# Block 14's last down product: from ahead of the last block's projection to behind it

## The chip, the cores and the metric

The kernel runs on one core of one Trainium2 chip. A core has five engines with instruction queues of their own: TensorE (PE in the profile, its weight loads PEld), VectorE (DVE), ScalarE (ACT), GpSimd (POOL) and SyncE (SP), which here issues nearly all DMA transfers. Each engine takes its instructions in the order in which the program wrote them. The metric is the device time of one execution in microseconds (us).

## The reference

A transformer block with adaptive layer norm, on x of 8 sequences with 1024 tokens of 512 features, all in float32:

```
mod = silu(cond) @ Wada + bada        # six vectors of 512 for each sequence
xm  = layernorm(x, g1, be1) * (1 + sc_a) + sh_a
x   = x + gt_a * (causal attention, 16 heads of 32, of xm @ Wqkv) @ Wproj + bproj, gated
xm  = layernorm(x, g2, be2) * (1 + sc_m) + sh_m
h   = gelu(xm @ W1 + b1)              # 2048 features
out = x + gt_m * (h @ W2 + b2)
```

The change touches only the order of the last three lines for two neighbouring stretches of tokens: the second layer of the MLP (W2) of one, and the projection and second norm of the next.

## The kernel before

A block is one half of a sequence, 512 tokens; there are 16 blocks, 0 to 15, and block 15 is the last. In each block the kernel computes k, q and v, attention, the projection ("proj"), the modulated second norm ("mt"), four up steps ("u", one quarter of W1 each) and the down steps ("d", W2). Attention of block w and the linear layers of its neighbours run in one window w of a plan: lists of steps for each window, built in a loop (L245 to L287). Two strands share TensorE: attention, written by `attend`, and the linear steps, written as Python generators that stop wherever they would have to wait.

The big products use Strassen's scheme in Winograd's form: seven products of half size for eight. For W2 the pieces of the weight are A11, A12, A22 and the sums S1 to S4 of them, which are kept in DRAM; the pieces of the hidden layer are B11, B12, B21, B22, overwritten in place by their differences. One product of the down step reads four weight tiles (128 x 512) and is 16 calls of `matmul` (L212), each 8 matmul instructions in the profile; a product of an up step is four calls. `DOWN_ORDER` (L305) splits the seven down products into parts:

```
DOWN_ORDER = (("A11", "S1"), ("S4", "A12"), ("S2",), ("S3", "A22"))
```

Part 3, the last, first takes S3 with B11, adds the earlier partial sums (`u_d`, `p_d` in the profile), and stores token rows 256 to 511 of the block; then it takes A22 with B21, adds S3's result (`u3`, in the buffer `p1`) to it, gates it, adds it to the residual `xr` and stores rows 0 to 255 (L1399 to L1418).

The order of the work is written out ahead by a planner inside the program: it keeps a reckoned time for each engine (`now`), for when data is written (`written`) and when buffers are left (`left`). `work` (L1507) lets that strand write its next instruction whose reckoned wait is the shortest; side strands stand ahead of the main one in a tie, in the order in which they began. The main strand runs the plan's steps one after the other (`linear`); a step named "beside" is started as a side strand, and the main one goes on with the next step at once. When the last block's attention is done, `drain` writes all that is left.

Weights come through a ring of eight tiles (`RING`, `fetch`, L351): the order in which they are asked for is fixed by the plan (`order`, made of `pieces_of`), and tile i is asked for on SP's queue once tile i - 8 has been released. Linear products share three PSUM banks.

The last block's projection (`project_out`, L1131) runs over four row tiles of 128 tokens: four calls each, the one for the attention's last quarter being the last. Each tile is gated and added to the residual on DVE, and its norm follows at once (`normalize_tile`, L672: statistics on DVE, the root and the normalising on ACT, giving `hat_m`). "mt" (`modulated`, L725) then transposes the normalised tiles on TensorE (L771), scales and shifts them from PSUM (L775, L781) into `xm_m`, and makes the sums T1 to T4 for the up step (`t_m`). The first up step of block 15 doesn't begin before block 14's down steps are written ("down done").

The plan of the final window, with late the down parts 1 to 3 of block 14:

```
plan[NB] = late[:-1] + [("beside", late[-1]), ("proj", n), ("mt", n)] + mlp_steps(n)
```

Of the kernel before, what the change touches and what calls it, by code (L numbers as in the profile page):

```python
# [22 lines left out]
def kernel(  # L23
# [46 lines left out]
    NQ = HD // D  # L70
# [20 lines left out]
    NB = len(blocks)  # L91
# [149 lines left out]


    def mlp_steps(n):
        return [("u", n, i) for i in range(NQ)] + [("d", n, part) for part in range(4)]

    plan = {
        -1: [("mod", 0), ("mod", 1), ("sums", "k", 0), ("norm_columns_a",), ("at", 0)]
# [6 lines left out]
    for w in range(1, NB):  # L254
        n = w - 1
        m = mlp_steps(n)
        even = blocks[n][1] == 0
        rows_a = [("rows", blocks[n][0], "a")] if even else []
        rows_m = [("rows", blocks[n][0], "m")] if even else []
        own = m[:1] + ([("load_xa", w + 2)] if w + 2 < NB else []) + m[1:3]  # L260
        own += [("norm_a", w + 2)] if w + 2 < NB else []
        if w == NB - 1:
            steps = late[:2] + rows_a + [("proj", n), ("mt", n)] + late[2:]
            steps += rows_m + own + m[3:5] + [("load_xr", w)]
            late = m[5:]
        else:

            steps = late + [("v", w)] + rows_a + [("proj", n), ("mt", n), ("k", w + 1)]
            if w > 3 and blocks[w][1]:
                steps = late[:-1] + rows_a + [("proj", n), ("mt", n)] + late[-1:] + [("k", w + 1)]  # L270
            if w == 2:
                steps = late + [("v", w), ("k", w + 1)] + rows_a + [("proj", n), ("mt", n)]
            if w == 1:
                steps = rows_a + [("k", w + 1), ("proj", n), ("mt", n)]
            early_v = [("v", w + 1)] if w > 2 and not blocks[w][1] else []
            steps += early_v + [("q", w + 1)] + rows_m + own
            at = [("at", w + 2)] if w + 2 < NB else []
            if blocks[w][1] == 0:

                steps += m[3:5] + [("load_xr", w)]  # L280
                late = m[5:6] + at + m[6:]
            else:
                steps += m[3:5] + [("load_xr", w)] + m[5:6] + at
                late = m[6:]
        plan[w] = steps
    n = NB - 1
    plan[NB] = late[:-1] + [("beside", late[-1]), ("proj", n), ("mt", n)] + mlp_steps(n)  # L287

    kept_sums = {}
    column_source = {"k": (Wqkv, 1), "q": (Wqkv, 0), "v": (Wqkv, 2)}  # L290
# [11 lines left out]


    ORDER = ("A11", "A12", "S2", "S1", "S3", "S4", "A22")
    DOWN_ORDER = (("A11", "S1"), ("S4", "A12"), ("S2",), ("S3", "A22"))  # L305
    AT = {"A11": (0, 0), "A12": (1, 0), "A22": (1, 1)}
    FULL = {"A11": (0, 0), "A12": (1, 0), "A21": (0, 1), "A22": (1, 1)}
    RAW = ((0, 0), (1, 0), (0, 1), (1, 1))
# [5 lines left out]
    def pieces_of(step):  # L314

        kind = step[0]
        if kind == "mod":
            return [(Wada, step[1], kh, fh) for kh, fh in RAW]
        if kind == "gates":
            return [(Wada, GATES[step[1]][0], kh, fh) for kh, fh in RAW]  # L320
        if kind == "beside":
            return pieces_of(step[1])
        if kind == "proj" and not by_quarters(step[1]):
            return [(Wproj, 0, k) for k in range(NC)]
        if kind == "d":
            return [
                (W2, i, *AT[a]) if a in AT else (W2, i, a)
                for a in DOWN_ORDER[step[2]]
                for i in range(NQ)
            ]  # L330
        if kind == "sums":
            return [(*source_of(step[1:]), kh, fh) for kh, fh in RAW]
        if raw_step(step):
            return []
        if kind in ("k", "q", "v", "u", "proj"):
            w, i = source_of(step)
            return [(w, i, *AT[a]) if a in AT else (w, i, a) for a in ORDER]
        return []
# [942 lines left out]
    def down(n, part):  # L1281
# [85 lines left out]
        if part == 0:  # L1367
            yield [("g", n, 0), ("g", n, 1), "prepared", ("row", "gbm", n)], []
            for i in range(NTT):
                add_to(residual[n][:, i, :], gate_rows["gbm"], [("row", "gbm", n)], [("xr", n, i)])  # L1370
            written["rowgb free"] = due([("xr", n, i) for i in range(NTT)])
            combine(nc.vector, "B12", "B12", "B11")
            bank, ps = yield from product("B11")
            got["u1"] = stage("p1", "p1")
            copy_out(got["u1"], bank, ps, [key("u1")])
            bank, ps = yield from product("B12")
            got["u5"] = stage("p5", "u4")
            copy_out(got["u5"], bank, ps, [key("u5")])
        elif part == 1:
            bank, ps = yield from product("B22")  # L1380
            got["v3"] = stage("v3", "y", 2)
            y_key("v3", True)
            combine_out(got["v3"], bank, ps, got["u5"], [key("u5")], [key("v3")])
            combine(nc.vector, "B22", "B22", "B12")
            combine(nc.gpsimd, "B11", "B22", "B11")
            bank, ps = yield from product("B21")
            y = stage("y11", "y", 2)
            y_key("y11", True)
            combine_out(y, bank, ps, got["u1"], [key("u1")], [key("y11")])
            combine(nc.gpsimd, "B21", "B21", "B22")  # L1390
            settle(n, 0, 0, y, key("y11"))
        elif part == 2:
            bank, ps = yield from product("B22")
            u2 = got["u2"] = stage("u2", "u2")
            combine_out(u2, bank, ps, got["u1"], [key("u1")], [key("u2")])
            v3 = got["v3"]
            add_to(v3, u2, [key("u2")], [key("v3")])
            settle(n, 0, 1, v3, key("v3"))
        else:  # L1399
            u2, u5 = got["u2"], got["u5"]  # L1400
            bank, ps = yield from product("B11")
            u3 = stage("u3", "p1")
            combine_out(u3, bank, ps, u2, [key("u2")], [key("u3")])
            add_to(u5, u3, [key("u3")], [key("u5")])
            settle(n, 1, 1, u5, key("u5"))
            store(n, 1)
            if n == NB - 1:
                yield from last_product(u3, next_pieces=[next(at) for _ in range(NQ)])
                return
            bank, ps = yield from product("B21")  # L1410
            y = stage("y21", "y", 2)
            y_key("y21", True)
            combine_out(y, bank, ps, u3, [key("u3")], [key("y21")])
            settle(n, 1, 0, y, key("y21"))
            store(n, 0)
            for q in range(NQ):
                hTs.pop((n, q))
            written["down done", n] = 0.0  # L1418


    def perform(step):
        kind = step[0]
# [4 lines left out]
        elif kind == "gates":  # L1427
            yield from gates(step[1])
        elif kind == "columns_m":
            columns_of["m"] = norm_columns("m", 3, 4, O_G2, O_BE2)  # L1430
        elif kind == "load_xa":
            x_pre[step[1]] = load_x(step[1])
        elif kind == "load_xr":
            start(load_xr(step[1]))
        elif kind == "norm_a":
            key = f"a{step[1]}"
            normalize(x_pre.pop(step[1]), key, [("x", key)] * NTT)
        elif kind == "at":
            n = step[1]
            guards = [("m used", n - 3)] if n > 2 else [("v done", 0)] if n == 2 else []  # L1440
            start(modulated(f"a{n}", *columns_of["a"], blocks[n][0], guards))
        elif kind == "beside":
            start(perform(step[1]))
        elif kind == "sums":
            sum_weights(step[1:])
        elif kind == "mt":
            n = step[1]
            guards = [("v done", n + 1)]
            start(modulated(f"m{n}", *columns_of["m"], blocks[n][0], guards))
        elif kind == "k":  # L1450
            if step[1] != 3:
                yield [("free for k", step[1])], []
            yield from project_T(step, kTs, kvp, "kT", lambda: None)
        elif kind == "q":
            yield from project_T(step, qTs, act, "qT", lambda: projected.add(step[1]))
        elif kind == "v":
            yield from project_v(step)
        elif kind == "preps":
            prepared[0] = [preparation(), 0.0]
            written["prepared up"] = written["prepared"] = NEVER  # L1460
        elif kind == "rows":
            gate_broadcasts(*step[1:])
        elif kind == "proj":
            yield from project_out(step[1])
        elif kind == "u":
            yield from up(step)
        elif kind == "d":
            yield from down(*step[1:])
# [620 lines left out]
```

## Time and profile before

| | before |
|---|---|
| median of 3 runs | 3505.3 us (3503.61 to 3505.68) |
| the profiled execution | 3501.11 us |
| its span, first to last instruction | 3499.4 us |
| mean granted TensorE clock | 0.998 |
| TensorE busy | 3441.3 us, 98% |
| VectorE, GpSimd, ScalarE busy | 63%, 60%, 35% |

A row of the timeline has the start in us from the span's start, the length in us, the engine, the line of the program, the operation, out<-in by the program's names, the shape, how many instructions were merged, and in brackets how long the engine was idle before and what released it. SPq is the DMA queue of SP. The granted clock is the share of full speed that the throttle granted to TensorE. A time in the chain of waits is a stretch of the work that ended last. Matmuls overlap, so that the ends of rows are modelled, and differences between starts are the better measure.

### The profile page before, as it was taken

What the parts mean: (1) busy time and instruction counts of PE and PEld (TensorE: products, weight loads), DVE (VectorE), ACT (ScalarE), POOL (GpSimd) and SP (SyncE); (2) the same over time, 40 slices, a digit from 0 to 9 for tenths busy, and PEclk for the clock granted to TensorE, in tenths of its full rate; (3) what the DMA queues carried; (4) which work ended last, traced back from release to release, by engine and by line L of the source; (5) the groups of instructions that cost most, each with busy time, mean ns of one, the idle gap of its engine ahead of it and who ended that gap; (6) DMA issues with size and microseconds to landing.
All of it is one profiled execution on the core that took longest, in us unless ns stands there. A gap on an engine that the chain in (4) does not pass through costs nothing. (4 is left out here: it accounts for less than half of the span.)

```text
span 3499.4 us, 122173 instructions
## 1 busy us (share of the span) xinstructions
PE 3441.3 (98%) x55101; PEld 1750.9 (50%) x55101; DVE 2203.8 (63%) x2808; ACT 1212.8 (35%) x1272; POOL 2113.7 (60%) x2255
## 2 busy tenths in 40 slices
PE   8999999999999999999999999999999999999999
PEld 4444455445544555445554455544555445554555
DVE  5775675565666566565666656665666656656573
ACT  2335333342343513335232442333423333323521
POOL 3667847667366663767627676375762857628640
PEclk9999999999999999999999999999999999999999
DMA  6763444535535455363554535545455454543344
GB/s 213 237 188 104 137 125 139 147 104 171 147 118 158 119 162 149 103 182 116 152 152 127 159 116 152 153 137 146 130 154 143 130 144 132 154 126 98 104 134 140
DMA packets 335580, 498.84 MB, mean 143 GB/s; under 512 B 27724, under 2 KB 184460, under 8 KB 331476
## 3 DMA queue, kind: packets, MB, share of 16 engines
q1 hardware_dynamic: 334944, 490.99, 47.8%
q8 instruction: 434, 7.11, 0.8%
q14 instruction: 86, 0.70, 0.1%
q10 hardware_dynamic: 116, 0.03, 0.0%
HBM read 432.13 MB, written 56.69 MB: 140 GB/s over the span
## 5 line engine op out<-in xcount | busy, mean ns | idle before, releaser
L1911 POOL TENSOR_TENSOR pT<-pT,pT 128x256 f32<-128x256 f32 (+3 forms) x1254 | 1224.7, 1012 | 238.9 <-PE po L1810 123.9
L1782 ACT ACTIVATE pT<-st 128x2048 f32<-128x2048 f32 x288 | 541.1, 1879 | 1017.5 <-PE st L1770 886.3
L217 PE MATMUL bank<-w,hT 128*32 128x256 f32 x14336 | 822.1, 380 | 0.0
L1694 DVE TENSOR_REDUCE mx<-sc 128x4 f32<-128x2048 f32 (+3 forms) x383 | 663.3, 1753 | 200.5 <-PE sc L1679 194.7
L217 PEld LDWEIGHTS bank<-w,hT 128*32 128x32 f32 x14336 | 448.0, 110 | 389.8 <-issue 109.7
L217 PE MATMUL bank<-xm_m,w 128*32 128x256 f32 x8192 | 497.4, 381 | 2.3 <-ACT p_u L197 1.0
L217 PE MATMUL bank<-t_m,w 128*32 128x256 f32 x6144 | 384.0, 380 | 2.5 <-DVE qT L208 1.4
L217 PEld LDWEIGHTS bank<-xm_m,w 128*32 128x32 f32 x8192 | 255.5, 110 | 227.3 <-issue 56.6
L1787 POOL TENSOR_SCALAR_AFFINE_SELECT pT<-pT 128x512 f32<-128x512 f32 x256 | 177.3, 710 | 313.7 <-ACT pT L1782 313.3
L1679 PE MATMUL sc<-kT,qT 32*128 32x512 f32 (+3 forms) x3064 | 328.0, 520 | 3.1 <-DVE mx L1694 1.8
L1691 DVE TENSOR_TENSOR sc<-sc,mask 128x1024 f32<-128x1024 f32 (+1 forms) x160 | 162.8, 1017 | 255.2 <-PE sc L1679 210.8
L1810 PE MATMUL po<-pT,v 128*32 128x512 f32 (+3 forms) x3048 | 301.7, 490 | 2.5 <-POOL pT L1787 2.3
L1770 PE MATMUL st<-qT,kT 32*128 32x512 f32 (+3 forms) x3072 | 302.7, 487 | 0.0
L217 PEld LDWEIGHTS bank<-t_m,w 128*32 128x32 f32 x6144 | 188.9, 110 | 178.8 <-issue 49.8
L217 PE MATMUL bank<-xm_a,w 128*32 128x256 f32 x3968 | 241.6, 380 | 2.4 <-ACT p_k L197 1.1
L1679 PEld LDWEIGHTS sc<-kT,qT 32*128 32x128 f32 x3064 | 129.2, 183 | 182.4 <-issue 82.4
L208 DVE TENSOR_TENSOR hT<-bank,u_u 128x512 f32<-128x512 f32 x186 | 126.0, 686 | 127.2 <-PE bank L217 126.5
L217 PE MATMUL bank<-t_a,w 128*32 128x256 f32 x2944 | 182.3, 380 | 1.4 <-ACT qT L204 0.9
L1885 POOL TENSOR_TENSOR qT<-top,rec 128x512 f32<-128x512 f32 x61 | 79.8, 1309 | 170.7 <-DVE rec L1857 167.8
L217 PE MATMUL bank<-w,qT 128*32 128x512 f32 (+1 forms) x1824 | 175.4, 515 | 3.7 <-DMA w<-in_L_cond_Wproj_dram 3.7
L1199 ACT ACTIVATE hT<-hT,cols 128x512 f32<-128x512 f32 x256 | 164.7, 711 | 40.7 <-DVE hT L208 27.4
L217 PEld LDWEIGHTS bank<-xm_a,w 128*32 128x32 f32 x3968 | 123.9, 110 | 101.3 <-issue 16.9
(262 smaller groups left out, 3657.1 us busy)
## 6 DMA issues: line engine op xcount, KB each, us to landing
w<-in_L_cond_W_dram SPq DMA_DIRECT2D x384, 256.0 KB
w<-kept_up_S SPq DMA_DIRECT2D x256, 256.0 KB
w<-kept_down_S SPq DMA_DIRECT2D x256, 256.0 KB
w<-kept_qkv_S SPq DMA_DIRECT2D x180, 256.0 KB
w<-in_L_cond_Wqkv_dram SPq DMA_DIRECT2D x147, 256.0 KB
hat_a<-in_x_dram SPq DMA_DIRECT2D x64, 256.0 KB
xr<-in_x_dram SPq DMA_DIRECT2D x32, 512.0 KB
out_dram<-xr SPq DMA_DIRECT2D x31, 512.0 KB
```

What stands on the lines that cost most here:

```text
L208: nc.vector.tensor_tensor(out, src, other, op)
L217: nc.tensor.matmul(ps[r, :], columns, rhs, start=start, stop=stop, skip_group_check=True)
L1199: nc.scalar.activation(hT[:, i, :], hT[:, i, :], AF.Gelu, bias=cols[:, O_B1 + f : O_B1 + f + 1])
L1679: nc.tensor.matmul(sc[:, j, c0 : c0 + w], qTs[n][r, gg, ts(qt, P)], keys_of(n, kh)[r, gg, :w], start=True, stop=True, skip_group_check=True,)
L1691: nc.vector.tensor_tensor(place, place, shape_of.to_broadcast(place.shape), ALU.add)
L1694: nc.vector.tensor_reduce(maxima[n, gg][:, kh, qt, :], sc[:, :, c0 : c0 + w], axis=AX.X, op=ALU.max)
L1770: nc.tensor.matmul(st[:, j, c0 : c0 + w], kT[r, gg, ts(k % NTT, P)], qT[r, gg, TB - w :], start=False, stop=True, skip_group_check=True,)
L1782: nc.scalar.activation(pT[:, :, :used], st[:, :, :used], AF.Exp, scale=scale)
L1787: nc.gpsimd.affine_select(diagonal, diagonal, pattern=[[0, HPG], [1, P]], compare_op=ALU.is_ge, fill=0.0, base=0, channel_multiplier=-1,)
L1810: nc.tensor.matmul(po[r, TB - w :], v[:, k % NTT, g * P + j * hd : g * P + (j + 1) * hd], pT[:, j, c0 : c0 + w], start=(k == 0), stop=last ...
L1885: nc.gpsimd.tensor_tensor(qTs[n][:, g, :], top, rec, ALU.mult)
L1911: nc.gpsimd.tensor_tensor(into, into, pT[:, j, c0 : c0 + w], ALU.add)
```

## The change

The last part of the down step is cut in two: part 3 keeps S3 with B11, and a new part 4 has A22 with B21. For all blocks but 14 the two parts stand next to each other in the plan, as they did inside part 3; the lists in the plan that were cut before their last item are cut before their last two. In the final window part 3 of block 14 is started beside the projection of block 15, as before; part 4 is started as a side strand only when the projection has been written and "mt", the transposes behind the second norm, has been started. The order of the weight tiles follows: S3's four, Wproj's four, A22's four, then the up step's, where it was S3's, A22's, Wproj's, the up step's. `beside` takes a list of steps now, which `both` runs one after the other.

```
     def mlp_steps(n):
-        return [("u", n, i) for i in range(NQ)] + [("d", n, part) for part in range(4)]
+        return [("u", n, i) for i in range(NQ)] + [("d", n, part) for part in range(5)]
...
             if w > 3 and blocks[w][1]:
-                steps = late[:-1] + rows_a + [("proj", n), ("mt", n)] + late[-1:] + [("k", w + 1)]
+                steps = late[:-2] + rows_a + [("proj", n), ("mt", n)] + late[-2:] + [("k", w + 1)]
...
     n = NB - 1
-    plan[NB] = late[:-1] + [("beside", late[-1]), ("proj", n), ("mt", n)] + mlp_steps(n)
+    plan[NB] = late[:-2] + [("beside", late[-2:-1]), ("proj", n), ("mt", n), ("beside", late[-1:])] + mlp_steps(n)
...
-    DOWN_ORDER = (("A11", "S1"), ("S4", "A12"), ("S2",), ("S3", "A22"))
+    DOWN_ORDER = (("A11", "S1"), ("S4", "A12"), ("S2",), ("S3",), ("A22",))
...
         if kind == "beside":
-            return pieces_of(step[1])
+            return [at for of in step[1] for at in pieces_of(of)]
...
-        else:
+        elif part == 3:
             u2, u5 = got["u2"], got["u5"]
             bank, ps = yield from product("B11")
             u3 = stage("u3", "p1")
...
             store(n, 1)
+            got["u3"] = u3
+        else:
+            u3 = got["u3"]
             if n == NB - 1:
                 yield from last_product(u3, next_pieces=[next(at) for _ in range(NQ)])
                 return
...
+    def both(steps):
+        for step in steps:
+            yield from perform(step)
...
         elif kind == "beside":
-            start(perform(step[1]))
+            start(both(step[1]))
```

## The prediction

> **What bounds the kernel now.** I read the page first, then the chain of waits, then TensorE's timeline around the place that the change touches, then the same place on the other engines and the DMA queue.
>
> ```profile
> span 3499.4 us, 122173 instructions
> PE 3441.3 (98%) x55101; PEld 1750.9 (50%) x55101; DVE 2203.8 (63%) x2808; ACT 1212.8 (35%) x1272; POOL 2113.7 (60%) x2255
> ```
>
> TensorE is busy for all but 58.1 us of the span. An edit that only moves its work can gain no more than the idle time, and the slow time, of the places that it touches. Before the junction of blocks 14 and 15 the order of steps is the same in both kernels: every list in the plan that was cut before its last item is now cut before its last two, and flattens to the same order; the four-part cost of a block is the same sum. So I look at the junction alone. The chain of waits, in its columns start, length, what:
>
> ```profile
> 3350.57 40.52 PE bank L217 x624
> ...
> 3391.11 0.70 DVE y L208
> ...
> 3393.77 1.51 ACT hat_m L691 x2
> 3395.32 2.40 PE bank L771 x13
> 3397.73 97.74 PE bank L217 x1792
> ```
>
> The chain is on TensorE up to 3391.1, leaves it for the norm of the last row tile (DVE, then ACT) and comes back at 3395.3; then 97.74 us of matmuls without a gap lead to the end. Whatever is gained before 3397.7 moves all that follows by as much. TensorE's own timeline (start, length, what, idle before):
>
> ```profile
> 3350.20 27.12 PE L217 MATMUL bank<-w,hT 128*32 128x256 f32 x496
> 3376.97 14.09 PE L217 MATMUL bank<-w,qT 128*32 128x512 f32 x128
> 3390.99 0.33 PE L771 MATMUL bank<-ident,hat_m 128*128 128x128 f32 x1
> 3391.66 0.33 PE L771 MATMUL bank<-ident,hat_m 128*128 128x128 f32 x1 [0.33 <-ACT hat_m L691]
> 3394.62 0.33 PE L771 MATMUL bank<-ident,hat_m 128*128 128x128 f32 x1 [2.63 <-ACT hat_m L691]
> 3395.32 2.40 PE L771 MATMUL bank<-ident,hat_m 128*128 128x128 f32 x13 [0.38 <-ACT hat_m L691]
> 3397.66 2.79 PE L217 MATMUL bank<-xm_m,w 128*32 128x256 f32 x32
> 3400.27 1.90 PE L217 MATMUL bank<-t_m,w 128*32 128x256 f32 x32
> 3402.00 3.63 PE L217 MATMUL bank<-xm_m,w 128*32 128x256 f32 x64
> 3446.89 48.52 PE L217 MATMUL bank<-w,hT 128*32 128x256 f32 x896
> ```
>
> The first row is block 14's last four products with W2 (A12, S2, S3, A22), run through without a pause although the last two were started "beside" the projection; the second is the projection. Then TensorE waits three times for normalised tiles: 0.33 + 2.63 + 0.38 = 3.34 us. And it is slow afterwards. In the stretches below the columns are length, TensorE busy, granted clock, DMA share, GB/s:
>
> ```profile
> 3395.00:3396.00 1.00, 0.68 (x6) 1.00 0.01 2
> 3396.00:3397.00 1.00, 1.00 (x7) 0.51 0.00 0
> 3397.00:3398.00 1.00, 1.00 (x8) 0.50 0.00 0
> 3398.00:3399.00 1.00, 1.00 (x16) 0.50 0.00 0
> 3399.00:3400.00 1.00, 1.00 (x20) 0.78 0.00 0
> ```
>
> Time lost to the clock there: 0.49 + 0.50 + 0.50 + 0.22 = 1.71 us. Idle and slow time make 5.05 us, the most that filling this hole can bring.
>
> **The change, part by part.** *Splitting the last part of the second layer.* For blocks 0 to 13 and 15 nothing lies between the two halves, so their order is unchanged; I take zero, and the cover isn't work but identity of the two orders.
>
> *The second half (A22 with B21) leaves the stretch ahead of the projection.* The 896 matmuls of the last row are seven products of the same kind: 48.52 / 7 = 6.93 us; less the modelled tail of the row, 6.9 us, or 0.43 us for each of the product's 16 calls of eight matmuls. So the projection starts at 3376.97 - 6.9 = 3370.1 and ends at 3384.1 instead of 3391.0. That needs its data 6.9 us earlier:
>
> ```profile
> 3358.38 5.55 SPq L362 DMA_DIRECT2D w<-in_L_cond_W_dram  x4
> 3365.28 5.51 SPq L366 DMA_DIRECT2D w<-in_L_cond_Wproj_dram  x4
> 3372.19 2.11 SPq L362 DMA_DIRECT2D w<-in_L_cond_W_dram  x2
> 3377.80 2.20 SPq L1250 DMA_DIRECT2D out_dram<-xr  x2
> 3390.24 1.24 SPq L362 DMA_DIRECT2D w<-in_L_cond_W_dram  x2
> 3365.74 0.29 DVE L1866 TENSOR_TENSOR qT<-top,rec 128x128 f32<-128x128 f32 x1
> 3372.65 0.69 DVE L167 TENSOR_TENSOR xr<-xr,p_d 128x512 f32<-128x512 f32 x1
> ```
>
> The ring has eight slots, so a weight tile is requested when the tile eight places earlier is released. Today A22's four tiles are requested from 3358.4 to 3363.9 (behind S2's release) and Wproj's four from 3365.3 to 3370.8. The two groups change places in the order, so Wproj takes the first times. For the landing I take a bound: the last weight request before the hole ends by 3391.5, and the DMA share is 0.01 in 3395 to 3396, so a tile lands within some 4 us. Wproj is there by 3363.9 + 4 = 3367.9, 2.2 us ahead of need; the last quarter of the attention output is there at 3366.0, 4.1 us ahead; DVE has finished S3's additions at 3373.3, and the projection's first row tile comes out seven of sixteen calls after its start, near 3376.3. Nothing waits: zero, between the bounds 0 and 4 us. The weights of the following up layer lose: four of them are today requested behind A22's release (3372.2 onward) and now behind Wproj's, at the projection's last row tile, near 3381 to 3384. With 4 us they are there at 3388, and the first is needed after 3394. Zero.
>
> *The second half fills the hole.* The norm's chain depends on the projection alone, so it moves by 6.9 us with it:
>
> ```profile
> 3388.27 0.81 ACT L691 ACTIVATE hat_m<-xr,offset_m,rstd_m 128x512 f32<-128x512 f32 x1
> 3390.80 0.80 ACT L691 ACTIVATE hat_m<-xr,offset_m,rstd_m 128x512 f32<-128x512 f32 x1
> 3393.77 1.50 ACT L691 ACTIVATE hat_m<-xr,offset_m,rstd_m 128x512 f32<-128x512 f32 x2
> 3396.13 2.42 ACT L781 ACTIVATE xm_m<-bank,shiftm,gainm 128x512 f32<-128x512 f32 x3 [0.86 <-PE bank L771]
> 3399.30 0.69 DVE L167 TENSOR_TENSOR t_m<-t_m,xm_m 128x512 f32<-128x512 f32 x1
> ```
>
> The four normalised tiles come 1.9 us before the projection's end, and 0.6, 3.5 and 4.3 us behind it. The hole behind it is thus 4.3 us, and 6.9 us of A22 stand ready. In what order they are written is settled by the kernel's planner: it takes whichever thread waits least, the transposes' first in a tie. By its own reckoning of the norm the tiles come at -1.3, 1.6, 4.4 and 5.2 us of the projection's end, later than in the trace, so it writes one transpose, three calls of A22, a transpose, six calls, a transpose, one call, then transposes with two calls and four calls put where a PSUM bank is not yet free. The price of such mixing shows where block 14's transposes were mixed with W2 products:
>
> ```profile
> 3212.02 0.33 PE L771 MATMUL bank<-ident,hat_m 128*128 128x128 f32 x1
> 3212.28 0.64 PE L217 MATMUL bank<-w,hT 128*32 128x256 f32 x8
> 3212.85 0.33 PE L771 MATMUL bank<-ident,hat_m 128*128 128x128 f32 x1
> 3214.75 1.97 PE L771 MATMUL bank<-ident,hat_m 128*128 128x128 f32 x14
> ```
>
> 14 transposes take 1.97 us, 0.14 each. One transpose and one call take 3212.85 - 3212.02 = 0.83 us, 0.26 more than 0.14 + 0.43: each change of kind costs 0.13 us. From the projection's end to the first product with a sum (T2), the after kernel runs 16 transposes (2.25), 16 calls (6.9), the first up product (four calls, 1.73) and some ten changes of kind (1.3): 12.2 us. Today that stretch takes 3400.27 - 3390.99 = 9.3 us, with 6.9 us of A22 ahead of the projection: 16.2 us. **The gain is 16.2 - 12.2 = 4.0 us.** The same from the other side: 3.34 idle + 1.71 slow clock - 8 more changes of kind at 0.13 = 4.0. Bounds: 5.1 if there are no more changes than today; 3.0 if the transposes wait as much for free banks as today's thirteen (2.40 against 13 x 0.14 = 1.8, so 0.6) and the planner mixes three times more.
>
> *What the half's own outcome is queued with.* Its DVE work is three instructions (bank plus S3's result, times the gate, into the residual) of 0.69 us, 2.1 us in all. It stood in DVE's idle time ahead of the projection; now it stands behind the sums for the up layer (last today at 3399.30). The sums themselves stand ahead of it by the planner's times, so T2 isn't delayed: after hat 4.3 us behind the projection, four evictions and two sums end near 3394.5, and TensorE wants T2 at 3396.3. Up's first partial product reuses the buffer of S3's result, so its copy out waits for the first of the three, near 3396; the bank it frees is wanted two products later. Zero, at most 1 us. The store of rows 0 and 1 of block 14 now stands on the DMA queue behind four more weight requests and ahead of the next layer's; with eight tiles (eight products, 13.8 us) in hand nobody waits for it.
>
> **The rivals.** *The clock stays low (3503.0).* If the slow 3.4 us isn't due to this hole, only the idle time less the changes of kind comes back: 3.34 - 1.04 = 2.3. For it: no single pause is longer than 2.63 us, and TensorE worked for 1 us in between. Against it: the fall follows the pauses at once, within 0.7 us. The Trainium skill, "TensorE: Matmul & The Clock Gate", section "What's actually happening", says that the clock halves after an idle window of about 3.4 us and recovers after about 3.4 us of sustained work; the trace agrees with half and with the 3.4 us of recovery, but taken literally, a pause of 2.63 us should not have cost anything, and the loss would have another source.
>
> *It doesn't do what it says (3505.3).* If all transposes are written ahead of A22, TensorE's queue keeps its order: it waits 3.34 us as now and A22 follows behind, 6.9 us later. The stretch is 16.2 us in both. It would take a planner that sees no wait at the second and third tile; it reckons 1.6 us and 4.4 us, so I hold it unlikely.
>
> *Slower (3511).* The Wproj requests get behind the store of block 14's rows 2 and 3 on the DMA queue. That store waits for the addition at 3372.65 + 0.69, takes 1.1 us to issue (2.20 for two), and Wproj's first tile lands at 3374.4 + 4 = 3378.4, against 3370.1: 8.3 us of waiting, another fall of the clock (1.7) and 4.0 gained elsewhere make +6.0. It decides once the projection starts later than 3374.1. Against it: the requests are written as S2 is released, before the store's addition exists.
>
> **How the numbers follow.** The profiled execution took 3501.11 us (span 3499.4 and 1.7 around it); less 4.0 it is 3497.1. The median of the three runs is 3505.3, 4.2 us above the profiled one, so I forecast 3501.3. Chances: 0.72 for this, 0.08 for the clock that stays low, 0.09 for no effect, 0.05 for the late weights, 0.06 for a larger gain from something that the trace of before doesn't show. 0.2% is 7.0 us, about what a measurement of this kernel can tell from no change, and more than the 5.05 us that the hole holds: faster 0.06, same 0.89, slower 0.05. The likeliest case alone gives 3500.2 to 3502.3 and, with the 1 us by which the runs differ, 3499.2 to 3503.3. The range takes in no effect and a run 0.7 above it: 3499.0 to 3506.0.
>
> **What would show it.** Right: the profile shows the projection starting near 3370 straight behind S3; matmuls of bank<-w,hT between the transposes; TensorE's idle time in the junction under 0.5 us; a granted clock of 1.0 to the end; the T2 product near 3396.3. Wrong: an idle stretch ahead of the projection (weights or attention late), a new pause between the transposes and the up layer (DVE's queue), or a different order in an earlier block, which would show as a different instruction count or a shift before 3350.

## The result

| | before | after |
|---|---|---|
| median of 21 runs each | 3505.3 us (3499.37 to 3514.14) | 3500.46 us (3491.1 to 3504.99) |
| ratio | | 0.9983, 95% interval 0.9976 to 0.9989 |
| the profiled execution | 3501.11 us | 3492.33 us |
| its span | 3499.4 us | 3490.6 us |

The kernel became 0.17% faster by the ratio, which is 6.0 us, with an interval of 3.9 to 8.4 us; the medians lie 4.8 us apart. The forecast was a gain of 4.0 us and a time of 3501.3. On the page of the changed kernel the span is 8.8 us shorter and TensorE is busy for 3.3 us less:

```profile
span 3490.6 us, 122172 instructions
PE 3438.0 (98%) x55101; PEld 1752.9 (50%) x55101; DVE 2204.5 (63%) x2809; ACT 1211.8 (35%) x1271; POOL 2112.5 (61%) x2255
```

DVE has one instruction more and ACT one less, since one of the last transposed tiles (`xm_m`) is now scaled on DVE. That is at the junction: up to the place where A22's product stood, TensorE, DVE, ACT and GpSimd run the same instructions in the same order in both traces.

The chain of waits no longer leaves TensorE at the junction (start, length, what):

```profile
3346.26 33.59 PE bank L217 x496
3379.84 0.26 PE bank L771
3380.10 1.43 PE bank L217 x24
...
3388.07 98.60 PE bank L217 x1824
```

TensorE's timeline of the changed kernel shows what stands where DVE and ACT stood in the chain before:

```profile
3345.03 1.22 PE L1838 MATMUL bank<-pT,ones 128*32 128x512 f32 x8
3345.89 20.22 PE L217 MATMUL bank<-w,hT 128*32 128x256 f32 x368
3365.75 14.10 PE L217 MATMUL bank<-w,qT 128*32 128x512 f32 x128
3379.78 0.33 PE L771 MATMUL bank<-ident,hat_m 128*128 128x128 f32 x1
3380.03 1.50 PE L217 MATMUL bank<-w,hT 128*32 128x256 f32 x24
3381.47 0.33 PE L771 MATMUL bank<-ident,hat_m 128*128 128x128 f32 x1
3381.72 2.80 PE L217 MATMUL bank<-w,hT 128*32 128x256 f32 x48
...
3385.28 0.77 PE L771 MATMUL bank<-ident,hat_m 128*128 128x128 f32 x5
3385.98 1.07 PE L217 MATMUL bank<-w,hT 128*32 128x256 f32 x16
3386.98 1.09 PE L771 MATMUL bank<-ident,hat_m 128*128 128x128 f32 x8
3388.00 1.93 PE L217 MATMUL bank<-w,hT 128*32 128x256 f32 x32
...
3391.48 1.91 PE L217 MATMUL bank<-t_m,w 128*32 128x256 f32 x32
```

No row has an idle time in brackets, and the clock is full throughout (length, TensorE busy, granted clock, DMA share, GB/s):

```profile
3379.78:3391.48 11.70, 11.70 (x178) 1.00 0.51 161
```

To compare kernels I measure the **junction**: from the start of the last product with ones to the start of the first product with t_m. In the kernel before, the first mark is this row of TensorE's timeline:

```profile
3349.35 1.22 PE L1831 MATMUL bank<-pT,ones 128*32 128x512 f32 x8
```

Before: 3400.27 - 3349.35 = 50.92 us. After: 3391.48 - 3345.03 = 46.45 us. The junction gives 4.47 us. The two profiled spans differ by 8.8 us, and the other 4.3 us stood at the first mark already. They are no effect of the change, since up to there the instructions and their order are the same. The lead of the changed execution comes and goes on the way: 1.3 us at 146 us, 4.6 at 156, 1.4 at 2630 (the same matmul starts at 2629.99 and at 2628.65), 4.3 at the first mark. Its largest step shows how. The kernel before, first the stretch's granted clock (third figure), then its timeline:

```profile
146.50:149.90 3.40, 3.33 (x14) 0.51 1.07 245
```

```profile
146.57 1.21 PE L1649 MATMUL bank<-kT,qT 32*128 32x512 f32 x1 [2.19 <-DVE mx L1666]
156.00 0.40 PE L1758 MATMUL st<-mrow,minus_ones 32*128 32x384 bf16 x8
```

The changed kernel, the same stretch and the same instructions:

```profile
146.50:149.90 3.40, 3.40 (x22) 1.00 1.09 286
```

```profile
145.25 0.69 PE L1656 MATMUL bank<-kT,qT 32*128 32x512 f32 x1 [2.39 <-DVE mx L1673]
151.37 0.40 PE L1765 MATMUL st<-mrow,minus_ones 32*128 32x384 bf16 x8
```

One execution fell to half clock behind a pause of 2.2 us, the other didn't behind 2.4 us (the last section says why). Ahead of it they are 1.32 us apart at the same instruction, behind it 4.63. Single executions of one kernel differ by such events, so below single times are not compared, only junctions within a trace, and the medians of null_split, one_piece and late_turns, which were run ten or eleven times.

### The profile page after: what moved, and what is told of

It reads as the page before. It is cut to its first block, busy times and chain, and to the rows that moved or that the text cites. A ratio compares the mean times of both kernels' runs of the same rounds, so it can differ in the third digit from the quotient of the medians.

```text
span 3490.6 us, 122172 instructions
## 1 busy us (share of the span) xinstructions
PE 3438.0 (98%) x55101; PEld 1752.9 (50%) x55101; DVE 2204.5 (63%) x2809; ACT 1211.8 (35%) x1271; POOL 2112.5 (61%) x2255
```

## The experiments

| kernel | first mark | T2 product | junction, us | longest pause in it, us | half clock behind it |
|---|---|---|---|---|---|
| before | 3349.35 | 3400.27 | 50.92 | 2.63 | yes |
| null_split | 3348.72 | 3399.39 | 50.67 | 2.64 | yes |
| both_ahead | 3347.74 | 3399.51 | 51.77 | 2.63 | yes |
| behind_turns | 3344.40 | 3396.02 | 51.62 | 2.56 | yes |
| fill_3, two executions | 3352.70, 3355.88 | 3402.38, 3405.55 | 49.68, 49.67 | 1.61, 1.60 | no |
| fill_7 | 3356.32 | 3406.00 | 49.68 | 0.19 | no |
| old_loads | 3352.94 | 3400.89 | 47.95 | 1.30 | no |
| after | 3345.03 | 3391.48 | 46.45 | none | no |
| both_behind | 3351.05 | 3397.49 | 46.44 | none | no |
| one_piece | 3348.98 | 3394.89 | 45.91 | none | no |
| late_turns | 3357.79 | 3403.37 | 45.58 | none | no |

**The cut without the move.** In null_split only the plan's line differs from the changed kernel:

```
-    plan[NB] = late[:-2] + [("beside", late[-2:-1]), ("proj", n), ("mt", n), ("beside", late[-1:])] + mlp_steps(n)
+    plan[NB] = late[:-2] + [("beside", late[-2:]), ("proj", n), ("mt", n)] + mlp_steps(n)
```

> The part is cut in two as in the changed kernel, but both halves run ahead of the projection, as before: every engine gets the instructions of the kernel before in the same order. I measure the junction from the start of the last product with ones (bank<-pT,ones) to the start of the first product with t_m: 50.92 us before, 46.45 after. My theory (all of the gain is the filled hole) expects 50.9, with the half clock behind the hole again, and no difference in the median. Rival 1 (the half clock falls there by chance, wherever a free-running window happens to lie): 50.9 or 49.2. Rival 2 (the cut itself or the code's place brings something): a median some 4 us below the kernel before.

The expectation overlooked one thing: the second half now takes its tiles from the ring only after the projection has, so the last projection multiplies by A22's tiles and A22's product by Wproj's, and the output is not the block's. The instructions of the engines and their order are those of before, and only the times are used here. Junction 50.67 us, ratio 1.0007 (0.9998 to 1.0016). The cut itself brings nothing; rival 2 falls.

In both_ahead part 3 takes all eight tiles, which puts both the tiles and their requests where they were before:

```
-    DOWN_ORDER = (("A11", "S1"), ("S4", "A12"), ("S2",), ("S3",), ("A22",))
+    DOWN_ORDER = (("A11", "S1"), ("S4", "A12"), ("S2",), ("S3", "A22"), ())
...
-            got["u3"] = u3
+            got["u3"], got["at"] = u3, at
...
-            u3 = got["u3"]
+            u3, at = got["u3"], got["at"]
```

and the plan's line is that of null_split.

> Cut in two as in the changed kernel, but both halves ahead of the projection and the weight tiles asked for in the old order: the instructions of the kernel before, in its order, on every engine. Theory: the hole and the half clock behind it are there again, junction (from the start of the last product with ones to the first product with t_m) 50.9 us against 46.45 of the changed kernel. Rival (the half clock behind the hole is chance): 49.2 us.

Its timeline, and behind it the stretches with the granted clock as the third figure:

```profile
3393.01 0.47 PE L771 MATMUL bank<-ident,hat_m 128*128 128x128 f32 x1 [2.63 <-ACT hat_m L691]
```

```profile
3395.00:3397.00 2.00, 2.00 (x13) 0.50 0.00 0
3397.00:3399.00 2.00, 2.00 (x24) 0.53 0.00 0
```

The hole and the half clock are there again. Here the half clock lasted twice as long, 6.8 us in place of 3.4, and began during the pause; the junction is 51.77, so what the hole costs varies by about 1 us (50.67 to 51.77 in the three kernels with the old order). That the half clock comes by chance at this place, the first rival, isn't borne out: four kernels of four with this pause show it.

**The hole filled, nothing moved.** fill_7 is the kernel before with a strand of useless calls:

```
+    def filler(calls):
+        yield [], [BANK]
+        bank = lin_bank()
+        for i in range(calls):
+            if i:
+                yield [], []
+            matmul(
+                banks[bank][:, :HB], qTs[NB - 1][:, 0, :P], gate_rows["gm"][:, :HB],
+                i == 0, i == calls - 1, [], bank,
+            )
+        live[bank] = False
+        left["l", bank] = now["PE"]
...
+        elif kind == "fill":
+            start(filler(step[1]))
...
-    plan[NB] = late[:-1] + [("beside", late[-1]), ("proj", n), ("mt", n)] + mlp_steps(n)
+    plan[NB] = late[:-1] + [("beside", late[-1]), ("proj", n), ("mt", n), ("fill", 7)] + mlp_steps(n)
```

> The kernel before, with seven useless calls (56 matmuls on data that is there, into a free bank, read by nobody) written as a side strand beside the transposes: they fill the wait for the norm and move nothing. If the half clock is the price of the hole, the clock stays at 1.0 and the stretch from the projection's end to the first product with t_m falls from 9.28 to about 8.2 us although TensorE has 3.0 us more to do; junction 49.8. If the low clock has another source, it stays, and the stretch grows to 9.9 us; junction 51.5.

From fill_7's timeline, and its granted clock from the projection's end to T2:

```profile
3399.92 1.93 PE L217 MATMUL bank<-row_gm,qT 128*32 128x256 f32 x32
3402.30 1.89 PE L771 MATMUL bank<-ident,hat_m 128*128 128x128 f32 x13 [0.19 <-ACT hat_m L691]
```

```profile
3397.97:3406.00 8.03, 7.81 (x107) 1.00 0.42 127
```

8.03 us for that stretch against 9.28 before, though TensorE has 3.0 us more to do. The norm comes no sooner: the last 13 transposes start 18.36 us behind the projection's start (3402.30 - 3383.94), and 18.35 us in the kernel before (3395.32 - 3376.97). From there T2 follows in 3.70 us, against 4.95 before. What went is the half clock, and it was worth 1.25 us. fill_3, the same with three calls, asks how long a pause it takes:

> The kernel before with three useless calls in place of seven: the first 1.3 us of the wait are filled, some 1.5 us ahead of the third transpose and 0.4 us ahead of the fourth stay idle. What it tells apart: whether a pause of 1.5 us is enough to bring the half clock (so far the junction showed it in four looks of four with a pause of 2.6 us, and in none of five without a pause above 0.2 us). With the half clock the junction is about 50.9 us, without it 49.2. I expect 49.2: no half clock.

> The same kernel once more, since a free-running window may lie differently: 49.2 us without the half clock, 50.9 or more with it. If one look has it and the other not, the pause of 1.5 us is near the bound and chance decides.

The first execution's timeline, and its stretch from the projection's end to T2:

```profile
3397.98 0.33 PE L771 MATMUL bank<-ident,hat_m 128*128 128x128 f32 x1 [1.61 <-ACT hat_m L691]
```

```profile
3394.35:3402.38 8.03, 6.01 (x74) 1.00 0.37 120
```

Both executions have a pause of 1.6 us and full clock, and the same 8.03 us: with 2.0 us still idle the junction is that of fill_7, since the norm's chain sets when the last 13 transposes can start, 18.35 us behind the projection's start here too. The expected 49.2 took all of the 1.71 us of slow time for lost; 1.25 us were. At full clock TensorE waits for a part of that time anyway: in fill_3 the first up product starts 1.87 us ahead of T2, not 1.73, and a gap of 0.2 us lies between two of the 13 transposes.

**Behind the projection, but not in the hole.** In behind_turns part 4 of block 14 waits for a mark that is set when the transposes are written:

```
+            if n == NB - 2:
+                yield ["transposed"], []
...
+        if key == f"m{NB - 1}":
+            written["transposed"] = 0.0
...
+    written["transposed"] = NEVER
```

> The changed kernel, but A22's product may only be written once all transposes are: it is behind the projection and doesn't fill the hole. My theory: TensorE waits 3.3 us for the norm as before, nothing is gained, junction 49.2 to 50.9 us (without and with the half clock). Rival (the gain comes from the projection's earlier start, or from its weights' earlier requests): 46.5.

Its timeline, and a stretch of its granted clock:

```profile
3382.77 0.47 PE L771 MATMUL bank<-ident,hat_m 128*128 128x128 f32 x1 [2.56 <-ACT hat_m L691]
3383.47 3.04 PE L771 MATMUL bank<-ident,hat_m 128*128 128x128 f32 x13 [0.23 <-ACT hat_m L691]
3386.44 8.02 PE L217 MATMUL bank<-w,hT 128*32 128x256 f32 x128
```

```profile
3386.00:3388.00 2.00, 2.00 (x19) 0.50 0.00 0
```

The projection starts as early as in the changed kernel, and the pause is 2.56 us as before; 13 transposes take 3.04 us and A22 7.85 by the starts (3394.29 - 3386.44) instead of 6.9, both in part at half clock. The junction is 51.62, 0.7 above the expected range, with a half clock that lasted 6.8 us as well. An earlier projection, with its weights asked for earlier, is worth nothing alone: the gain is the filling.

**More behind the projection.** both_behind moves S3's product too:

```
+    plan[NB] = late[:-2] + [("proj", n), ("mt", n), ("beside", late[-2:])] + mlp_steps(n)
```

> S3's product goes behind the projection too: 13.8 us of work stand ready for a hole of 4.3 us behind the projection. Theory: only the hole can be filled, so the second 6.9 us bring nothing, junction 46.0 to 47.0 us. Rival 1 (each product moved behind gains as much again): 43 or less. Rival 2 (the projection now comes before its attention rows and weights, which were 4.1 and 2.2 us ahead of need in the prediction's sum): 48 or more, with an idle stretch ahead of the projection.

The row of its timeline behind the last transpose:

```profile
3387.11 8.84 PE L217 MATMUL bank<-w,hT 128*32 128x256 f32 x160
```

46.44 us, the changed kernel's 46.45. Twelve calls of S3 fill the hole, as twelve of A22 did in the changed kernel; the other four and all of A22 run behind the transposes. Both rivals fall; the projection doesn't wait either, although it starts 6.9 us earlier still.

**The old order of requests.** old_loads has the changed kernel's plan with both_ahead's `DOWN_ORDER` and taking of tiles.

> The changed kernel's order of matmuls with the old order of weight requests: S3's four tiles, A22's four, Wproj's four, so that Wproj's come 6.9 us later and A22's eight slots are held until behind the projection. Theory: Wproj's requests leave some 5 us ahead of use at first and arrive just in time or up to 1 us late: junction 46.4 to 47.5. Rival (the exchange of the requests is needed, the prediction's slower case): the projection waits 2 us or more, junction above 48.4, half clock behind it possible.

From its timeline, and from its chain of waits:

```profile
3377.03 12.22 PE L217 MATMUL bank<-w,qT 128*32 128x512 f32 x112 [1.30 <-DMA w<-in_L_cond_Wproj_dram]
```

```profile
3372.32 4.66 DMA w<-in_L_cond_Wproj_dram
```

The projection's first two calls run at 3373.65, 0.88 us each, and the third waits until 3377.03, 1.6 us late by the starts; the junction is 47.95, between the two expectations. So the exchanged order of requests is part of the change's gain, 1.5 of the 4.47 us, but its lack doesn't turn the sign.

**Better mixtures.** one_piece starts A22's strand ahead of the transposes':

```
+    plan[NB] = late[:-2] + [("beside", late[-2:-1]), ("proj", n), ("beside", late[-1:]), ("mt", n)] + mlp_steps(n)
```

> A22's product is started ahead of the transposes, so that it runs in one piece and the 16 transposes follow. If each change of kind costs 0.13 us, eight changes fewer save 1.0 us, and waits for banks and for the last eviction give some back: 45.9 to 46.7 us for the junction against 46.45. Rival (the mixing is what hides the evictions): transposes, evictions and sums stand in a row behind the product, and the junction is 47.5 or more.

late_turns leaves the plan and lets the first transpose wait for all four tiles:

```
-            yield [("hat", key, 0), *guards], [BANK]
+            whole = range(NTT) if key == f"m{NB - 1}" else range(1)
+            yield [*(("hat", key, t) for t in whole), *guards], [BANK]
```

> The changed kernel, but the first transpose waits for the fourth normalised tile, so that TensorE changes between A22's calls and transposes six times, not ten, and two groups of calls still cover the evictions. By 0.13 us for a change: 0.5 us less than the changed kernel, junction 45.9 us; in the median no difference from it that can be told, about 0.998 of the kernel before. Rival (a change of kind costs nothing when both kinds stand ready): 46.4.

From the timeline of late_turns:

```profile
3392.24 5.54 PE L217 MATMUL bank<-w,hT 128*32 128x256 f32 x96
3397.71 1.09 PE L772 MATMUL bank<-ident,hat_m 128*128 128x128 f32 x8
3398.73 1.07 PE L217 MATMUL bank<-w,hT 128*32 128x256 f32 x16
3403.37 1.91 PE L217 MATMUL bank<-t_m,w 128*32 128x256 f32 x32
```

one_piece has 45.91 and 0.9984 (0.9975 to 0.9993), late_turns 45.58 and 0.9978 (0.9968 to 0.9987). Fewer changes of kind are cheaper: late_turns was written with four of them, not the six of the expectation, so six less than the changed kernel, and saved 0.87 us, 0.15 for each. In one_piece eight changes fewer saved only 0.54 us: the up layer's first product starts 2.07 us ahead of T2 and not 1.73, which the expected waits for the evictions would do; no run takes that apart. By one trace each both beat the changed kernel; by the medians neither can be told from it.

## Why the prediction was right

*The start of the projection* came 6.9 us earlier as summed: from the first mark to its start 27.62 us before (3376.97 - 3349.35), 20.72 after (3365.75 - 3345.03).

*The written order* is the predicted one call for call: a transpose, three calls, a transpose, six, a transpose, one, five transposes, two calls, eight transposes, four calls.

*The stretch from the projection's end to T2* was put at 12.2 us and took 11.70. The mis-sized term is the transposes, 0.14 us each or 2.25 in all: eight of them with one change of kind take 1.02 us and five with one change 0.70, which makes 0.11 each, 1.8 in all. The row from which the 0.14 came (14 in 1.97 us) holds a change of kind too, and a wait for the eviction of a bank, which the kernel before shows on the weight loads of its last four transposes:

```profile
3216.06 0.42 PEld L771 LDWEIGHTS bank<-ident,hat_m 128*128 128x128 f32 x4 [0.23 <-ACT xm_m L781]
```

With 11.70 the working gives 16.2 - 11.7 = 4.5 us, the junction's 4.47.

*The two losses*, idle time and half clock, are told apart by fill_7 and fill_3: with the pause cut to 1.6 us or less, the clock stays full and the stretch is 1.25 us shorter although changes of kind were added. So the sum from the other side, 3.34 + 1.71 - 1.04 = 4.0, came near by luck: with 1.25 for the clock it gives 3.55. Of the 0.9 us between that and 4.47, the two waits seen in fill_3, 0.14 and 0.2 us, are a part, since the changed kernel has neither; no run takes the rest apart. The rival that the clock stays low fell; "it doesn't do what it says" fell with the written order.

*What is queued behind* cost nothing, as said, but was larger than said. The timeline of the changed kernel, DVE, GpSimd and the DMA queue:

```profile
3389.65 0.69 DVE L167 TENSOR_TENSOR t_m<-t_m,xm_m 128x512 f32<-128x512 f32 x1
3390.26 0.68 DVE L208 TENSOR_TENSOR y_d<-bank,u_d 128x512 f32<-128x512 f32 x1
3390.97 1.06 DVE L167 TENSOR_TENSOR y_d<-y_d,row_gm 128x512 f32<-128x512 f32 x1
3392.07 1.66 DVE L167 TENSOR_TENSOR xr<-xr,y_d 128x512 f32<-128x512 f32 x1
3389.69 1.79 POOL L170 TENSOR_TENSOR t_m<-xm_m,t_m 128x512 f32<-128x512 f32 x1 [30.34 <-DVE t_m L793]
3391.45 5.89 POOL L170 TENSOR_TENSOR xr<-xr,row_gbm 128x512 f32<-128x512 f32 x4
3354.07 5.51 SPq L366 DMA_DIRECT2D w<-in_L_cond_Wproj_dram  x4
```

The second half's three DVE instructions took 3.4 us, not 2.1: those with both inputs in SBUF ran 1.06 and 1.66 us beside GpSimd's rows, the one that reads a bank 0.68. That GpSimd's work is the cause isn't shown: the first DVE row, with both inputs in SBUF and beside a GpSimd row as well, took 0.69. The first of the three was done at 3390.94, ahead of the up layer's copy, and TensorE waited for none.

*The weights' lead* was larger than summed, 5.3 us and not 2.2, though a tile can take 4.66 us to land (old_loads) and not 4. The sum asks for all four tiles at the projection's start; in old_loads two calls ran before the third waited for its own tile, 1.6 us. In the changed kernel the requests leave 6.9 us earlier against the first mark (9.04 us behind it, 15.93 in old_loads), so 6.9 - 1.6 = 5.3 us are left at that call. With the old order the lead was gone, so the rival on late weights was the right place to look, though its mechanism, a store ahead of the requests, did not occur: the store stands behind all eight of them.

*The size in the medians* is 4.8 us. The three kernels with the old order average 51.1 us at the junction, 4.7 above the changed one. The interval, 3.9 to 8.4 us, takes that in; the traces show at most 5.3 (both_ahead against the changed kernel), and for a gain above that no run here has a cause.

## What to carry to other kernels

A wait of two or three microseconds on TensorE can cost twice, once as idle time and once in the clock behind it; look for work with no tie to the wait that can be written behind its start, as much as the hole holds: more brought nothing here (both_behind). Move the work's weight requests with it, and check what the engines that take its results have to do at the new place. When a change is worth a tenth of a percent, measure its stretch between two marks in the trace, because whole executions differ by more than that from events elsewhere.

## What the runs showed of the hardware

A pause far shorter than the stretch of half clock behind it was enough: pauses of 2.6 us brought 3.4 or 6.8 us of half clock in four kernels of four, pauses of 1.6 us in two executions none. What decides is not the pause alone but where it lies. In each trace the granted clock changes only on a grid of 3.41 us: in the kernel before, half clock begins at 146.54 and 3396.03 us, which is 952 times 3.4133 us apart; in null_split at 397.25, 2984.55 and 3394.15, 758 and 120 times. The grid lies differently in each execution. The rows are windows of the grid (length, TensorE busy, granted clock, DMA share, GB/s): one of the kernel before, two of the changed kernel (its grid counted back from 3489.33, where its only half clock begins), two of both_ahead.

```profile
143.12:146.54 3.42, 1.26 (x10) 1.00 1.08 213
```

```profile
140.85:144.26 3.41, 1.99 (x14) 1.00 1.07 232
144.26:147.68 3.42, 2.44 (x22) 1.00 1.09 218
```

```profile
3388.65:3392.06 3.41, 1.39 (x10) 1.00 0.70 242
3392.06:3395.48 3.42, 2.24 (x10) 0.50 0.31 107
```

The pause of 2.2 us at 146 us lay in one window, which was idle for 2.16 us, and half clock followed. The pause of 2.4 us was split over two windows, idle for 1.42 and 0.98 us, and the clock stayed full. Counted over the twelve traces, from where the record of the clock begins (20 to 27 us), all 34 windows at full clock with 2.05 us idle or more were followed by half clock, and none with less than 1.6 us; of the 24 in between 4 were. The ends of matmuls are modelled, so these bounds are rough. At the junction one window was idle for 2.38 us in the kernel before and for 2.93 in null_split, and the half clock behind it lasted one window. In both_ahead and behind_turns the pause was split, 2.02 and 1.18, 1.71 and 1.49 us: half clock began inside the pause and lasted two. What makes it last two is open, for behind the pause at 146 us it lasted two as well, with TensorE idle for only 0.03 us in the first. fill_3 had 1.51 and 1.56 us in a window, of 2.0 us idle in all; its full clock doesn't show that a pause of 1.6 us is safe wherever the grid lies.

The Trainium skill, "TensorE: Matmul & The Clock Gate", section "What's actually happening", gives an idle window of about 3.4 us that runs freely as the condition. The traces agree with a window of 3.41 us that runs freely; they do not agree that all of it must be idle, since 2.05 us were enough each time.
